# Gathered float32 rows of A, added on VectorE, for every other step of the last chunk of a graph layer

## The chip, the cores and the metric

The kernel runs on one core of one Trainium2 chip. The engines are written as the profile has them: PE is TensorE (PEld its weight loads), DVE is VectorE, ACT is ScalarE, POOL is GpSimd, SP is SyncE, which here only issues DMAs. The metric is the device time of one execution in microseconds; lower is better. The time before is 2595.76 us, the median of 3 runs (2591.33 to 2597.96).

## The reference

12500 nodes with 64 features each, 212500 edges sorted by their destination node `dst`, one weight per edge. The first layer's matrix `eW1` has 129 rows: 64 for the row node, 64 for the column node, one for the weight. H is 128.

```python
h = jnp.maximum(_layernorm(x, axis=-1), 0.0)
# row = src, col = dst, dist = edge_weight1
edge_in = jnp.concatenate([h[row], h[col], dist], axis=1)
e = jax.nn.silu(edge_in @ eW1 + eb1)
e = jax.nn.silu(e @ eW2 + eb2)
agg = jax.ops.segment_sum(e, row, num_segments=h.shape[0])
node_in = jnp.concatenate([h, agg], axis=1)
out = x + jax.nn.silu(node_in @ nW1 + nb1) @ nW2 + nb2
```

The edge layer's first product splits into a table A of h times the first 64 rows of `eW1` (taken by `src`), a table B of h times the next 64 rows (taken by `dst`), and the weight's row. The sums run over `src`, while the edges come sorted by `dst`.

## The kernel before, in words

**Tables.** `products` (L578) forms the rows of A and of B for four nodes per partition at a time, 25 times. A is written to DRAM (`ta`) as three bfloat16 parts whose sum is the float32 row (L591 to L601), B as float32 (`tb`, L594). `hd` keeps h, transposed, for the node layer (L586). This work, the "feed", is cut into pieces by `yield` and dealt out between the pieces of the next stage.

**Sorting the edges by source.** The nodes lie in 100 buckets of 125 (bucket is `src` mod 100). `send_all` takes the edges in blocks of 1024: `count` (DVE, L306 to L329) finds each edge's place in its bucket, `send` (L331 on) forms B plus the weight's part for each edge on PE (L349), copies it to SBUF on ACT (L356), and POOL scatters it by indirect DMA, 128 rows at a time, into a DRAM buffer `q` (L370). A row of `q` has 144 words: 128 of data and 16 with the edge's place in its bucket, plus one (a zero row has place zero). The edges are cut into 11 chunks; a chunk's part of `q` can only be read when all its scatters have landed. Zeros are written into the next chunk's part from ACT's queue.

**Reading back.** A batch is four buckets of one chunk: in the first chunk one step, in the ten others two steps, g = 0 and g = 1. A step handles four tiles of 128 edges. `fetch` (L405) is emitted four batches ahead, right after the `one` operation of a batch's last step, and issues on SP's queue: the tile `qt` of edges (L415, 576 KB), the rows of A for the four buckets, `a3` (L420), and in the last chunk the node layer's inputs `xr` and `hrn` (L105, L206); POOL adds a bias to `xr` (L204). The tile pool of `qt` has four buffers, so SP's issue waits until the batch four earlier has been read.

A step is a row of small functions:
- `s_lr` (PE, L438) spreads the place of each edge over the partitions; `s_one_t` (DVE, L443) compares it with the partition number, which gives a one-hot matrix `oneT`;
- `s_pt` (PE) transposes the edge rows into PSUM (L452) and adds the three parts of A times `oneT` (six matmuls, L459); ACT applies SiLU (L463);
- `s_bias` (ACT, L485), `s_p2` (PE, L491; ACT, L495): the second layer;
- `s_one` (DVE, L472) builds the one-hot matrix the other way round, and `s_seg` (PE, L505) sums with it;
- `s_add` (DVE, L516) adds the batch's sums to `aggT`.

In the last chunk the node layer follows each batch (`nodes`: PE L216, L219, L225, ACT L221, DVE L228 with `os`, SP L105).

**The order.** The work of PE, DVE, ACT and SP stands in the order in which the program emits it. In iteration k the emission is `s_pt(k+1)`, `s_add(k-2)`, `s_one_t(k+2)`, `s_bias(k+1)`, `s_p2(k)`, `s_one(k)`, `s_seg(k-1)`, `s_lr(k+3)`, with pieces of sending, feed and node layer at the four places marked `None` in `turn` (L523). POOL's order is left to the framework's scheduler.

Of the kernel before, what the change touches and what calls it, by code (L numbers as in the profile page):

```python
# [28 lines left out]
F32 = mybir.dt.float32  # L29
F16 = mybir.dt.float16  # L30
BF16 = mybir.dt.bfloat16
I32 = mybir.dt.int32
AF = mybir.ActivationFunctionType
OP = mybir.AluOpType
# [4 lines left out]
P = 128  # L39
# [7 lines left out]
G = 4  # L47
# [12 lines left out]
def tile_gnn(ctx: ExitStack, tc: tile.TileContext, x, src, dst, ew, eW1, eb1, eW2, eb2, nW1, nb1, nW2, nb2, out):  # L60
    nc = tc.nc
    N, D = x.shape
    H = eW2.shape[0]
    E = src.shape[0]
    assert D == 64 and H == P and N % L == 0
    NB = N // L
# [6 lines left out]
    const = ctx.enter_context(tc.tile_pool(name="const", bufs=1))  # L73
    dram = ctx.enter_context(tc.tile_pool(name="dram", bufs=1, space=DRAM))
# [47 lines left out]
    nc.gpsimd.iota(nodes_i, pattern=[[1, L]], base=1, channel_multiplier=0)  # L122
    nodes1 = const.tile([P, L], F32, name="nodes1")
    nc.vector.tensor_copy(nodes1, nodes_i)
    w1 = const.tile([P, 2, H], F32, name="w1")
    w1n = const.tile([P, H], F32, name="w1n")
    for a in range(2):
# [24 lines left out]
    same = const.tile([P, 1], F32, name="same")  # L152
# [11 lines left out]

    ta = dram.tile([P * NB, 3 * H], BF16, name="ta")
    tb = dram.tile([P * NB, H], F32, name="tb")
    rows = dram.tile([NP, 2, 2, BLK], BF16, name="rows")

    tb0 = dram.tile([P * NE, H], F32, name="tb0")
# [2 lines left out]
    def product(s, hr, ps, tag, to):  # L172

        abs_ = []
        for a in range(2):

            half = slice(a * D, (a + 1) * D)
            ab = ps.tile([P, G // 2, H], F32, name="ab", tag=tag)
            for i in range(G // 2):
                nc.tensor.matmul(ab[:, i], hr[half, i, :], w1[half, s, :], start=True, stop=True)  # L180
            abs_.append(ab)
        for a in range(2):
            nc.scalar.copy(to.rearrange("l (i a) h -> l a i h", a=2)[:, a], abs_[a])
# [16 lines left out]
    def nodes_in(B, sb):  # L200
        b = B * G
        xr = sb.tile([L, G, D], F32, name="xr")
        rows16(nc.sync.dma_start, xr, x_rows[:, b : b + G, :])
        nc.gpsimd.tensor_tensor(xr, xr, nb2b[:L, None, :].to_broadcast([L, G, D]), op=OP.add)  # L204
        hr = sb.tile([P, G // 2, P], F32, name="hrn")
        nc.sync.dma_start(hr, hd[:, b // 2 : b // 2 + G // 2, :])  # L206
        return xr, hr
# [31 lines left out]
    with ExitStack() as work:  # L239
# [165 lines left out]
        def fetch(i):  # L405
            if i >= len(batches):
                return
            c, B, n = batches[i]
            assert pending[c] == 0
            while B not in done_a:  # L410
                next(feed)
            q = chunks[c][-1]
            at = B * G * n * P
            qt = ld2.tile([P, G * most, W], F32, name="qt")
            nc.sync.dma_start(  # L415
                qt[:, : G * n, :].rearrange("p j w -> p (j w)"),
                q[at : at + G * n * P, :].rearrange("(p j) w -> p (j w)", p=P),
            )
            a3 = ld2.tile([P, G, 3, H], BF16, name="a3")
            nc.sync.dma_start(  # L420
                a3.rearrange("l b s f -> l b (s f)"), ta_buckets[:, B * G : B * G + G]
            )
            batch[c, B] = [qt, a3, None]
            if c == len(chunks) - 1:
                node_in[B] = nodes_in(B, ndp[0])

        def of(k):

            c, B, n, g = steps[k]
            return batch[c, B], [((g * G + t) % n * G + (g * G + t) // n, (g * G + t) // n) for t in range(G)]  # L430

        def s_lr(k):
            (qt, _, _), tiles = of(k)
            loc = qt.rearrange("p j w -> p (j w)").bitcast(BF16)
            lr = mm.tile([P, G, P], F32, name="lr", tag="mm")
            for t, (j, _) in enumerate(tiles):
                at = 2 * (j * W + H) + 1
                nc.tensor.matmul(lr[:L, t, :], loc[:, at : at + 1].to_broadcast([P, L]), identb, start=True, stop=True)  # L438
            st[k] = {"lr": lr}

        def s_one_t(k):
            oneT = wk.tile([L, G, P], BF16, name="oneT")
            nc.vector.tensor_scalar(oneT, st[k].pop("lr")[:L], part1[:L, :], None, op0=OP.is_equal)  # L443
            st[k]["oneT"] = oneT

        def s_pt(k):

            (qt, a3, _), tiles = of(k)
            oneT = st[k].pop("oneT")
            pt = mm.tile([P, G, P], F32, name="pt", tag="mm")  # L450
            for t, (j, _) in enumerate(tiles):
                nc.tensor.matmul(  # L452
                    pt[:, t, :], qt[:, j, :H], ident, is_transpose=True, start=t == 0, stop=False, skip_group_check=True
                )
            for b, same in itertools.groupby(range(G), lambda t: tiles[t][1]):
                same = list(same)
                cols = slice(same[0], same[-1] + 1)
                for i in range(3):
                    nc.tensor.matmul(  # L459
                        pt[:, cols, :], a3[:L, b, i, :], oneT[:, cols, :], start=False, stop=i == 2, skip_group_check=True  # L460
                    )
            e1 = wk.tile([P, G, P], F32, name="e1")
            nc.scalar.activation(e1, pt, AF.Silu)  # L463
            st[k]["e1"] = e1
# [52 lines left out]
            if c == len(chunks) - 1:  # L517
                tails.append(nodes(B, *node_in.pop(B), mm, ndp[1], "mm"))

        tails, node_in = [], {}  # L520


        turn = [  # L523
# [34 lines left out]
        def first_rows(g):  # L558

            hr = turned(x0, g)  # L560
            yield
            got = fp.tile([P, G, H], F32, name="got")
            product(1, hr, mm, "mm", got)
            yield
            nc.sync.dma_start(tb0.rearrange("(p j) f -> p j f", j=NE)[:, g : g + G, :], got)
            yield
# [11 lines left out]
        def products(b0, g, xs):  # L578

            assert b0 in ready  # L580
            b = b0 + g
            hr = turned(xs, g)
            yield
            rows_a = fp.tile([P, G, H], F32, name="rows_a")
            product(0, hr, mm, "mm", rows_a)
            nc.sync.dma_start(hd[:, b // 2 : (b + G) // 2, :], hr)  # L586
            yield
            got = fp.tile([P, G, H], F32, name="got")
            product(1, hr, mm, "mm", got)
            parts = fp.tile([P, G, 3, H], BF16, name="parts")  # L590
            nc.scalar.copy(parts[:, :, 0, :], rows_a)  # L591
            yield
            nc.vector.tensor_tensor(rows_a, rows_a, parts[:, :, 0, :], op=OP.subtract)
            nc.sync.dma_start(tb_buckets[:, b : b + G, :], got)  # L594
            done_b.append(b // G)
            yield
            nc.scalar.copy(parts[:, :, 1, :], rows_a)
            yield
            nc.vector.tensor_tensor(parts[:, :, 2, :], rows_a, parts[:, :, 1, :], op=OP.subtract)
            yield  # L600
            nc.sync.dma_start(ta_buckets[:, b : b + G, :], parts.rearrange("p b s f -> p b (s f)"))  # L601
            done_a.append(b // G)
            yield
# [348 lines left out]
```

## Time and profile before

| | |
|---|---|
| median of 3 runs | 2595.76 us |
| the profiled execution | 2590.2 us, its span 2588.4 us |
| busy: PE, PEld | 2205.0 us (85%), 2041.8 us (79%) |
| busy: DVE, ACT, POOL | 2034.8 us (79%), 1246.9 us (48%), 1736.8 us (67%) |
| mean granted clock of PE | 0.926 |
| DMA over the span | 577.23 MB, 223 GB/s |
| POOL L370 scatters | 1661, mean 1022 ns |
| DVE L443 oneT, L472 one, L516 aggT | 525 of 744 ns, 525 of 670 ns, 250 of 667 ns |
| PE L438 lr, L459 products with A | 2100 of 225 ns, 3600 of 245 to 273 ns |

The span is the time from the first to the last recorded instruction of one execution; that execution's own time is 1.8 us longer. Matmuls overlap in PE, so a group's mean duration is longer than the step from one matmul to the next; the time that PE is held by some work is read from the starts in the timeline. "Idle before, releaser" names what ended an engine's idle time. A line of the timeline has start, duration, engine, line, operation, output and inputs with shapes, and in brackets the idle time before it.

### The profile page before, as it was taken

How to read it: one execution, taken by the hardware profiler on the slowest of the kernel's cores; microseconds unless marked ns; L12 is line 12 of the kernel's file. 1: busy time of each engine (PE TensorE's matmuls, PEld its weight loads, DVE VectorE, ACT ScalarE, POOL GpSimd, SP SyncE). 2: the span in 40 equal slices, each digit the busy share in tenths (PEclk: the TensorE clock that was granted, in tenths of full speed). 3: DMA queues.
4: the chain of work that ended last, by engine and by line, in shares of the span. 5: the costliest groups of instructions: out<-in, count | busy, mean ns of one | idle time of the engine just before them, and what ended most of it. 6: DMA issues, size and time to landing. Idle time of an engine off the chain costs nothing.

```text
span 2588.4 us, 60017 instructions
## 1 busy us (share of the span) xinstructions
PE 2205.0 (85%) x21814; PEld 2041.8 (79%) x21814; DVE 2034.8 (79%) x3464; ACT 1246.9 (48%) x2687; POOL 1736.8 (67%) x1729
## 2 busy tenths in 40 slices
PE   2456777988998998999899799889889999997997
PEld 1345667977987987888788799889879889996996
DVE  5877987987987887888788799879879889973442
ACT  2344634544554554555455455445545455553443
POOL 3675777777777777777677777777767777772000
PEclk7556888998999999999999899999989999998999
DMA  8787778669768767866966877786696667655441
GB/s 202 216 246 263 254 234 271 217 204 269 237 210 247 252 219 227 267 216 218 272 227 211 240 248 237 220 260 228 211 274 228 215 203 235 230 169 174 166 150 54
DMA packets 257977, 577.23 MB, mean 223 GB/s; under 512 B 51202, under 2 KB 110580, under 8 KB 257469
## 3 DMA queue, kind: packets, MB, share of 16 engines
q1 hardware_dynamic: 185096, 384.91, 45.7%
q0 software_dynamic: 54144, 123.04, 13.1%
q10 hardware_dynamic: 18434, 65.37, 11.4%
q8 instruction: 175, 2.87, 0.5%
q14 instruction: 128, 1.04, 0.1%
HBM read 361.44 MB, written 211.67 MB: 221 GB/s over the span
## 4 chain that ended last, share of the span: by engine, by line
PE 40%; DMA 23%; DVE 13%; POOL 7%; issue 6%; ACT 2%; SPq 1%; DVEq 0%; ACTq 0%; POOLq 0%
DMA q<-qs,to 14%; PE seg L505 10%; PE p L491 9%; POOL q L370 7%; PE pt L459 7%; PE pt L452 5%; DVE misc L317 5%; PE qp L349 4%; PE lr L438 3%; DMA bc<-rows 2%; DVE oneT L443 2%; DMA bb<-rows 2%; DVE one L472 2%; DMA pick<-in_edge_weight_dram 2%; DVE own L322 2%
## 5 line engine op out<-in xcount | busy, mean ns | idle before, releaser
L370 POOL DMA_INDIRECT q<-qs,to x1661 | 1697.4, 1022 | 602.7 <-issue 397.5
L463 ACT ACTIVATE e<-pt 128x512 f32<-128x512 f32 x525 | 313.7, 598 | 835.8 <-PE pt L459 769.6
L505 PE MATMUL seg<-one,e 128*128 128x125 f32 x4200 | 581.4, 282 | 54.7 <-DVE aggT L516 42.5
L491 PE MATMUL p<-w,e 128*128 128x128 f32 x4200 | 587.2, 284 | 5.3 <-ACT p L485 5.3
L317 DVE TENSOR_TENSOR_SCAN misc<-oh,misc 100x342 f32<-100x342 f16 (+1 forms) x623 | 579.7, 930 | 9.3 <-PE misc L341 1.2
L505 PEld LDWEIGHTS seg<-one,e 128*128 128x128 f32 x4200 | 524.4, 196 | 68.5 <-ACT p L485 27.7
L491 PEld LDWEIGHTS p<-w,e 128*128 128x128 f32 x4200 | 527.9, 197 | 31.0 <-issue 8.4
L443 DVE TENSOR_SCALAR oneT<-lr,part 125x512 bf16<-125x512 f32 x525 | 390.8, 744 | 111.1 <-PE lr L438 109.0
L459 PE MATMUL pt<-oneT,a 125*128 125x256 bf16 (+1 forms) x3300 | 443.0, 273 | 0.1
L452 PE MATMUL pt<-ident,qt 128*128 128x128 f32 x2100 | 332.0, 282 | 73.4 <-DVE oneT L443 73.4
L356 ACT COPY qs<-qp 128x512 f32<-128x512 f32 x416 | 229.2, 587 | 320.3 <-PE qp L349 225.7
L472 DVE TENSOR_TENSOR one<-nodes,qt 128x500 f32<-128x500 f32 x525 | 351.7, 670 | 0.7 <-PE seg L505 0.5
L459 PEld LDWEIGHTS <-a 125*128 125x128 bf16 x3300 | 318.7, 100 | 35.5 <-issue 1.0
L322 DVE TENSOR_TENSOR own<-misc,oh 100x342 f16<-100x342 f32 (+1 forms) x623 | 320.0, 514 | 21.6
L495 ACT ACTIVATE e<-p 128x512 f32<-128x512 f32 x525 | 314.1, 598 | 18.6 <-PE p L491 18.0
L485 ACT COPY p<-b2f 128x512 f32<-128x512 f32 x525 | 312.5, 595 | 0.1
L349 PE MATMUL qp<-win,pick 50*128 50x128 f32 x3322 | 260.7, 299 | 60.6 <-DMA pick<-in_edge_weight_dram 34.5
L349 PEld LDWEIGHTS qp<-win,pick 50*128 50x128 f32 x3322 | 220.4, 200 | 92.9 <-issue 71.5
L452 PEld LDWEIGHTS pt<-ident,qt 128*128 128x128 f32 x2100 | 228.3, 144 | 79.0 <-DVE oneT L443 76.3
L516 DVE TENSOR_TENSOR aggT<-aggT,seg 128x500 f32<-128x500 f32 x250 | 166.9, 667 | 94.2 <-PE seg L505 93.9
L438 PE MATMUL lr<-identb,qt 128*125 128x128 bf16 x2100 | 213.3, 225 | 30.6 <-DMA qt<-q 25.3
L438 PEld LDWEIGHTS <-qt 128*125 128x125 bf16 x2100 | 186.4, 139 | 42.1 <-DMA qt<-q 31.5
(121 smaller groups left out, 1086.3 us busy)
## 6 DMA issues: line engine op xcount, KB each, us to landing
qt<-q SPq DMA_DIRECT2D x250, 576.0 KB
a<-ta SPq DMA_DIRECT2D x275, 384.0 KB
q<-zeros ACTq DMA_DIRECT2D x30, 1638.0 KB
bb<-rows SPq DMA_DIRECT2D x208, 224.0 KB
bc<-rows SPq DMA_DIRECT2D x208, 128.0 KB
q<-qs,to POOLq DMA_INDIRECT x1661
win<-tb SPq DMA_DIRECT2D x416, 24.0 KB
ta<-parts SPq DMA_DIRECT2D x25, 384.0 KB
```

The costliest lines, as they stand in the source:

```text
L317: nc.vector.tensor_tensor_scan(run[:, :m], oh[:, cols], nil.to_broadcast([NB, m]), carry.get(c, -1.0), op0=OP.add, op1=OP.add)
L322: nc.vector.tensor_tensor(own[:, cols], run[:, :m], oh[:, cols], op=OP.mult)
L349: nc.tensor.matmul(qps[a][:, t, :], pick[half, t * P : (t + 1) * P], win[half, :], start=True, stop=True)
L370: i = nc.gpsimd.indirect_dma_start(out=q[:], out_offset=bass.IndirectOffsetOnAxis(ap=to[:k, t : t + 1], axis=0), in_=qs[:k, t - t0, :], in ...
L438: nc.tensor.matmul(lr[:L, t, :], loc[:, at : at + 1].to_broadcast([P, L]), identb, start=True, stop=True)
L443: nc.vector.tensor_scalar(oneT, st[k].pop("lr")[:L], part1[:L, :], None, op0=OP.is_equal)
L452: nc.tensor.matmul(pt[:, t, :], qt[:, j, :H], ident, is_transpose=True, start=t == 0, stop=False, skip_group_check=True)
L459: nc.tensor.matmul(pt[:, cols, :], a3[:L, b, i, :], oneT[:, cols, :], start=False, stop=i == 2, skip_group_check=True)
L472: nc.vector.tensor_tensor(one.rearrange("p (b j) l -> p b j l", j=n), nodes1[:, None, None, :].to_broadcast(wide), loc[:, tiles[0][1] : ti ...
L491: nc.tensor.matmul(p2[:, t, :], e1[:, t, :], w2, start=False, stop=t == G - 1, skip_group_check=True)
L495: nc.scalar.activation(e2, p2, AF.Silu)
L505: nc.tensor.matmul(item[2][:, b, :], e2[:, t, :], one[:, t, :], start=j < G, stop=j >= G * (n - 1))
```

## The change

For the last chunk, step g = 1 of each of its 25 batches gets the rows of A in another way.

- `products` also writes the float32 rows of A to a DRAM table `taf`. So that `rows_a` stays whole until that write has read it, the difference goes into a new tile `rest`; the tiles `got` and `rest` have two buffers (`got` had three).
- Two constants, `four_i` and `four`, are set up at the start.
- `fetch`, in the last chunk, adds two DVE operations on the location column of the tile that it has just asked for (`place`, then `idx`, the row numbers in `taf` of four tiles of edges), and four indirect DMAs on POOL, each of which gathers 128 rows of 512 bytes into `rows_of_a`.
- For such a step `s_lr` emits nothing, `s_one_t` adds `rows_of_a` to the edge rows in place on DVE, and `s_pt` only transposes.

Step g = 0 of each batch, and all other chunks, stay as they are.

```diff
--- before.py
+++ after.py
@@ -122,6 +122,10 @@
     nc.gpsimd.iota(nodes_i, pattern=[[1, L]], base=1, channel_multiplier=0)
     nodes1 = const.tile([P, L], F32, name="nodes1")
     nc.vector.tensor_copy(nodes1, nodes_i)
+    four_i = const.tile([P, G], I32, name="four_i")
+    nc.gpsimd.iota(four_i, pattern=[[1, G]], base=-NB, channel_multiplier=0)
+    four = const.tile([P, G], F32, name="four")
+    nc.vector.tensor_copy(four, four_i)
     w1 = const.tile([P, 2, H], F32, name="w1")
     w1n = const.tile([P, H], F32, name="w1n")
     for a in range(2):
@@ -164,6 +168,7 @@
 
     ta = dram.tile([P * NB, 3 * H], BF16, name="ta")
     tb = dram.tile([P * NB, H], F32, name="tb")
+    taf = dram.tile([P * NB, H], F32, name="taf")
     rows = dram.tile([NP, 2, 2, BLK], BF16, name="rows")
 
     tb0 = dram.tile([P * NE, H], F32, name="tb0")
@@ -423,6 +428,30 @@
             batch[c, B] = [qt, a3, None]
             if c == len(chunks) - 1:
                 node_in[B] = nodes_in(B, ndp[0])
+                if n > 1:
+
+                    k = steps.index((c, B, n, n - 1))
+                    _, tiles = of(k)
+                    idx = ndp[0].tile([P, G], I32, name="idx")
+                    place = ndp[0].tile([P, G], F32, name="place")
+                    b0 = tiles[0][1]
+                    loc = qt[:, : G * n, H : H + 1].rearrange("p (j b) w -> p b (j w)", b=G)[:, b0 : b0 + G // n]
+                    wide = [P, G // n, n]
+                    at = place.rearrange("p (b j) -> p b j", j=n)
+                    nc.vector.tensor_scalar(at, loc, 1.0, float(NB), op0=OP.max, op1=OP.mult)
+                    nc.vector.scalar_tensor_tensor(
+                        idx.rearrange("p (b j) -> p b j", j=n), at, float(B * G),
+                        four[:, b0 : b0 + G // n, None].to_broadcast(wide), op0=OP.add, op1=OP.add,
+                    )
+                    rows_of_a = ndp[0].tile([P, G, H], F32, name="rows_of_a")
+                    for t in range(G):
+                        nc.gpsimd.indirect_dma_start(
+                            out=rows_of_a[:, t, :],
+                            out_offset=None,
+                            in_=taf[:],
+                            in_offset=bass.IndirectOffsetOnAxis(ap=idx[:, t : t + 1], axis=0),
+                        )
+                    gathered[k] = rows_of_a
 
         def of(k):
 
@@ -431,6 +460,9 @@
 
         def s_lr(k):
             (qt, _, _), tiles = of(k)
+            if k in gathered:
+                st[k] = {}
+                return
             loc = qt.rearrange("p j w -> p (j w)").bitcast(BF16)
             lr = mm.tile([P, G, P], F32, name="lr", tag="mm")
             for t, (j, _) in enumerate(tiles):
@@ -439,6 +471,12 @@
             st[k] = {"lr": lr}
 
         def s_one_t(k):
+            if k in gathered:
+                (qt, _, _), tiles = of(k)
+                n = steps[k][2]
+                q = qt[:, : G * n, :H].rearrange("p (j b) w -> p b j w", b=G)[:, tiles[0][1] : tiles[0][1] + G // n]
+                nc.vector.tensor_tensor(q, q, gathered[k].rearrange("p (b j) w -> p b j w", j=n), op=OP.add)
+                return
             oneT = wk.tile([L, G, P], BF16, name="oneT")
             nc.vector.tensor_scalar(oneT, st[k].pop("lr")[:L], part1[:L, :], None, op0=OP.is_equal)
             st[k]["oneT"] = oneT
@@ -446,13 +484,14 @@
         def s_pt(k):
 
             (qt, a3, _), tiles = of(k)
-            oneT = st[k].pop("oneT")
             pt = mm.tile([P, G, P], F32, name="pt", tag="mm")
             for t, (j, _) in enumerate(tiles):
                 nc.tensor.matmul(
-                    pt[:, t, :], qt[:, j, :H], ident, is_transpose=True, start=t == 0, stop=False, skip_group_check=True
+                    pt[:, t, :], qt[:, j, :H], ident, is_transpose=True, start=t == 0,
+                    stop=k in gathered and t == G - 1, skip_group_check=True,
                 )
-            for b, same in itertools.groupby(range(G), lambda t: tiles[t][1]):
+            oneT = st[k].pop("oneT", None)
+            for b, same in [] if k in gathered else itertools.groupby(range(G), lambda t: tiles[t][1]):
                 same = list(same)
                 cols = slice(same[0], same[-1] + 1)
                 for i in range(3):
@@ -517,7 +556,7 @@
             if c == len(chunks) - 1:
                 tails.append(nodes(B, *node_in.pop(B), mm, ndp[1], "mm"))
 
-        tails, node_in = [], {}
+        tails, node_in, gathered = [], {}, {}
 
 
         turn = [
@@ -559,7 +598,7 @@
 
             hr = turned(x0, g)
             yield
-            got = fp.tile([P, G, H], F32, name="got")
+            got = fp.tile([P, G, H], F32, name="got", bufs=2)
             product(1, hr, mm, "mm", got)
             yield
             nc.sync.dma_start(tb0.rearrange("(p j) f -> p j f", j=NE)[:, g : g + G, :], got)
@@ -583,20 +622,22 @@
             yield
             rows_a = fp.tile([P, G, H], F32, name="rows_a")
             product(0, hr, mm, "mm", rows_a)
+            nc.sync.dma_start(taf.rearrange("(l b) f -> l b f", b=NB)[:, b : b + G, :], rows_a)
             nc.sync.dma_start(hd[:, b // 2 : (b + G) // 2, :], hr)
             yield
-            got = fp.tile([P, G, H], F32, name="got")
+            got = fp.tile([P, G, H], F32, name="got", bufs=2)
             product(1, hr, mm, "mm", got)
             parts = fp.tile([P, G, 3, H], BF16, name="parts")
             nc.scalar.copy(parts[:, :, 0, :], rows_a)
             yield
-            nc.vector.tensor_tensor(rows_a, rows_a, parts[:, :, 0, :], op=OP.subtract)
+            rest = fp.tile([P, G, H], F32, name="rest", bufs=2)
+            nc.vector.tensor_tensor(rest, rows_a, parts[:, :, 0, :], op=OP.subtract)
             nc.sync.dma_start(tb_buckets[:, b : b + G, :], got)
             done_b.append(b // G)
             yield
-            nc.scalar.copy(parts[:, :, 1, :], rows_a)
-            yield
-            nc.vector.tensor_tensor(parts[:, :, 2, :], rows_a, parts[:, :, 1, :], op=OP.subtract)
+            nc.scalar.copy(parts[:, :, 1, :], rest)
+            yield
+            nc.vector.tensor_tensor(parts[:, :, 2, :], rest, parts[:, :, 1, :], op=OP.subtract)
             yield
             nc.sync.dma_start(ta_buckets[:, b : b + G, :], parts.rearrange("p b s f -> p b (s f)"))
             done_a.append(b // G)
```

## The prediction

> **What bounds the kernel now.** I first read the busy time by stretch (columns: length, then busy us and instruction count of PE, PEld, DVE, ACT, POOL; then granted PE clock, DMA share, GB/s).
>
> ```profile
> 200.00:220.00 20.00, 6.52 (x52) 5.44 (x52) 9.94 (x17) 5.67 (x16) 8.38 (x8) 0.50 0.89 311
> 1000.00:2000.00 1000.00, 900.89 (x9118) 841.99 (x9119) 846.67 (x1428) 496.28 (x1062) 747.02 (x738) 0.96 0.76 238
> 2300.00:2340.00 40.00, 27.29 (x264) 26.18 (x262) 14.66 (x27) 14.90 (x30) 30.55 (x32) 0.87 0.33 108
> 2340.00:2588.00 248.00, 228.09 (x1951) 205.89 (x1951) 95.34 (x157) 103.18 (x204) 19.03 (x26) 0.96 0.43 140
> ```
>
> POOL's scatters run at one per 1.27 us (0.97 busy, 0.30 "issue"), which is a busy share of 0.76; it has 0.75 in the middle and 0.76 just before 2340. So scatter issue paces the kernel until 2340. From there PE is busy 92%, and POOL and DVE have room: the edited stretch is bound by PE. In the first stretch shown POOL is at half its pace with DMA at 0.89; I come back to it.
>
> Next, the timeline at the seam to the last chunk, and what SP's queue waits for (window 2300 to 2590):
>
> ```profile
> 2307.56 0.16 DVE L361 SCALAR_TENSOR_TENSOR to<-misc,bkE 128x5 int32<-128x5 f32 x1 [1.96 <-DMA q<-qs,to]
> 2307.64 0.67 DVE L472 TENSOR_TENSOR one<-nodes,qt 128x500 f32<-128x500 f32 x1
> ...
> 2313.02 0.67 DVE L472 TENSOR_TENSOR one<-nodes,qt 128x500 f32<-128x500 f32 x1
> ...
> 2326.24 1.05 PE L505 MATMUL seg<-one,e 128*128 128x125 f32 x8
> ...
> 2341.29 0.32 SPq L415 DMA_DIRECT2D qt<-q  x1
> ...
> 2345.71 0.50 PEld L438 LDWEIGHTS <-qt 128*125 128x125 bf16 x4 [18.61 <-DMA qt<-q]
> ```
> ```profile
> SPq L415 <- DVE one L472: 110.3, 24, 6.1
> SPq L415 <- DMA q<-qs,to: 30.9, 1, 30.9
> ```
>
> The `one` at 2313.02 belongs to the step after which the load for batch 0 of the last chunk (I write B0) is emitted. That load sits in SP's queue 30.9 us until the last scatter has landed, is issued at 2341.29, and its data release PE at 2345.71: 4.42 us. Meanwhile PE and DVE work on through three more batches, to 2327.3. In later rounds SP issues the load at once when `one` ends.
>
> Then one batch of the PE-bound stretch:
>
> ```profile
> 2407.60 0.68 DVE L516 TENSOR_TENSOR aggT<-aggT,seg 128x500 f32<-128x500 f32 x1 [1.54 <-PE seg L505]
> ...
> 2408.20 0.74 DVE L443 TENSOR_SCALAR oneT<-lr,part 125x512 bf16<-125x512 f32 x1
> ...
> 2408.86 0.67 DVE L472 TENSOR_TENSOR one<-nodes,qt 128x500 f32<-128x500 f32 x1
> ...
> 2409.59 0.34 SPq L415 DMA_DIRECT2D qt<-q  x1
> ...
> 2413.05 0.39 PE L438 MATMUL lr<-identb,qt 128*125 128x128 bf16 x4
> ...
> 2413.28 0.61 PE L452 MATMUL pt<-ident,qt 128*128 128x128 f32 x4
> ...
> 2413.73 0.82 PE L459 MATMUL pt<-oneT,a 125*128 125x256 bf16 x6
> ...
> 2414.38 1.06 PE L491 MATMUL p<-w,e 128*128 128x128 f32 x8
> ```
>
> Loads follow each other 8.76 us apart (2400.83, 2409.59): that is the round of a batch.
>
> **What is removed from PE.** By starts in those lines, four lr take 0.23 us (2413.05 to 2413.28) and six products with A 0.65 (2413.73 to 2414.38): 0.88 us per batch, 22 us over 25 batches. PE's round would become 7.88. DVE gives up one oneT (0.74) for an add of 128x512 f32; the nearest rows, one and aggT, have 0.67, and I take that. This is the whole possible gain.
>
> **What is added, and where it queues.** After the load, fetch now puts two small DVE operations that read the location column of the tile just being loaded. The rows u (0.15) and to (0.16) are the nearest: 0.31 us of work. But they wait for the load to land, and DVE takes its work in the order written: in the first pair of lines above `to` waits 1.96 us for a DMA, and `one` starts right behind it. So everything behind these two stands still for the whole load: os, oneT, one, aggT and the new add of the next two steps; PE waits for oneT, and the next load waits for the `one` that comes last in this list. Issue, landing and DVE's work make a closed ring, which does not exist now.
>
> The ring's length: two small ones 0.31, os 0.42, oneT 0.74, two one 1.34, aggT 0.68, new add 0.67 = 4.16. DVE's starts lie about 0.08 closer than its durations (2408.20 to 2408.86 for 0.74), six times: 3.68, plus 0.06 from one's end to the issue: about 3.75 us. To this comes the load, call it L.
>
> L in the trace, by the bytes that queue q1 had moved from just before the issue (0.59 MB is the tile). Windows 2400.8 to 2403.5, to 2403.75, without scatters; then 2301.7 to 2305, to 2305.5, with scatters beside it:
>
> ```profile
> q1 hardware_dynamic: 118, 0.54, 62.1%
> q1 hardware_dynamic: 151, 0.62, 64.0%
> ...
> q1 hardware_dynamic: 107, 0.49, 61.2%
> q1 hardware_dynamic: 166, 0.67, 65.2%
> ```
>
> Without scatters 0.59 MB is there at 2403.66, 2.83 us after the issue at 2400.83; with them at 2305.28, 3.56 after 2301.72. At the seam it was there at 2344.39 and PE went at 2345.71, so the end signal takes 1.32. L is 4.15 alone and 4.88 beside scatters. The gathers are such neighbours: four per batch at 1.27 us, after the xr add on POOL, about 2 to 7 us after a landing, while the next load is in flight from 3.75 to 8.4. No gather is in this trace; from below it costs nothing (4.15), from above I double the scatters' surcharge (5.6). I take 4.7, near the scatter row, since most of the load is overlapped and the rows are a little smaller.
>
> The ring is then 3.75 + 4.7 = 8.45 us, against 8.76 now and 7.88 for PE alone. So in the steady rounds a third of the gain is left: 0.31 us.
>
> A rule against the row: the Trainium skill, "DMA: Bandwidth & Descriptors", section "Anatomy of one DMA — SWDGE (gpsimd) path", fits a DMA by 2.0 us plus its bytes at 436 GB/s, 3.35 us for this tile (my estimate from it, for another path than this load's). By that the ring would be 7.1 us, hidden under PE's 7.88, and the change of the total about -5 us; the trace's 4.42 and 4.15 speak against it.
>
> **The seam.** DVE now stops behind the `one` of 2313.02 until 2345.7. PE comes as far as the lr three steps ahead, about 2318.2, and the work it did from there to 2327.3 is left for afterwards, 9 us. From 2345.7 the rounds are serial: 0.31 + oneT 0.67 + one 0.6 + aggT 0.6 + oneT 0.67 + one 0.67 puts the next issue at 2349.3 and its landing at 2354.0; the two small ones, five more operations and 4.7 give 2362.3; then 2370.5, 2378.7 (rounds of 8.2, no os yet). The transposes of batch B2 start after the small ones and oneT, at 2379.8, against 2363.8 now: 16.0 us late. PE's half clock after the gap (0.50 in the rows until 2350) is paid before and after alike.
>
> From there 20 rounds with a load each win 0.31: -6.2. The last three batches have no load to wait for and win PE's part: -2.4. Sum for the last chunk: 16.0 - 6.2 - 2.4 = +7.4 us.
>
> POOL's own work is covered: four gathers and xr are 5.8 us of an 8.4 us round, and each is used three batches later.
>
> **The early part.** 25 writes of A's f32 table (256 KB each) join SP's queue ahead of hd; behind each stand the bc, bb, win and pick loads. From 76 to 320 us DMA moved 59.49 MB at 244 GB/s; 6.4 MB more is 26 us if all of it were bound there, none if covered. POOL is short of work only around 160 to 240 (8.38 in the row above, against 15.3 at its pace), with some 7 of the 25 writes; I take half their DMA time, 7 x 1.05 / 2, about +4. Two buffers for got in place of three, and the new tile rest, only matter if a tb write is slow (one wait of 7.5 us in the trace); they stay in the range. The two constants cost 0.2 us at the start, covered by its loads.
>
> **Sum.** +7.4 + 4 = +11.4 us. On the profiled execution (2590.2, span 2588.4) that is 2601.6; that execution lies 5.6 below the median of the runs, 2595.76, so the forecast is 2607.2.
>
> **Rivals.**
> 1. The gathers crowd the load: L 5.6, ring 9.35. The seam becomes 16.0 + 4 x 0.9 = 19.6, twenty rounds +11.8, -2.4, +4: +33, 2629. For it: 512 more packets of only 512 bytes in each round. Against: scatters added only 0.73.
> 2. The gathers are harmless: L 4.15, ring 7.90, level with PE. 16.0 - 2.2 - 17.2 - 2.4 + 4: -2, 2594.
> 3. Faster: DVE's queue isn't held, because the two small ones find their tile landed or stand behind other work. Then no ring and no seam: -22 + 4 = -18, 2577.8. It decides only if the load is shorter than what DVE has to do ahead of them; the trace has nothing between `one` and the issue but 0.06 us, so I give it little.
> 4. The table writes cost the full 26: 2629, from a DMA share already at 0.9; against it, POOL is short of work in few stretches.
> That a gathered step is skipped silently I rule out: its tile is entered at least five steps before lr is built for it.
>
> **Chances.** The forecast, L from 4.4 to 5.0 (2600 to 2615): 0.50. Rival 1: 0.15. Rival 2: 0.15. Rival 3: 0.15. Rival 4: 0.05. What a measurement can tell from no change is 0.3%, 7.8 us: below 2588 or above 2603.5. Rival 3 gives faster, 0.15. Rival 2 and the lower part of the forecast (0.08) are the same, 0.23. The rest, 0.62, is slower. The range leaves out rival 3 and a little above rivals 1 and 4: 2589 to 2634.
>
> **What would show it.** DVE idle of about 4 to 5 us per batch before the place operation, ended by DMA qt<-q; one of about 32 us at the seam; loads 8.2 to 8.7 apart; PE no longer dense after 2350 but waiting for DVE oneT; and the last scatter landing within 0 to 10 us of 2341. If PE stays dense with rounds of 7.9, the ring is wrong; if the rounds are as said and the total still differs, the early part is.

## The result, and the profile after

The changed kernel takes 2597.1 us (median of 22 runs, 2589.65 to 2602.59). The kernel before takes 2590.43 us in the same comparison (22 runs, 2587.09 to 2597.96). The ratio is 1.002 with a 95% interval of 1.0011 to 1.0028: slower, by 5 us (the two medians lie 6.7 apart), and inside the 0.3% that the prediction called no change. The profiled execution took 2596.03 us, its span is 2594.3 us against 2588.4.

The last scatter, after which no stretch of the two kernels is paced by POOL any more, cuts the span in two. It starts at 2339.20 us before and at 2350.52 us after:

```profile
2339.20 0.89 POOL L370 DMA_INDIRECT q<-qs,to  x1 [0.31 <-issue]
```
```profile
2350.52 0.89 POOL L375 DMA_INDIRECT q<-qs,to  x1 [0.31 <-issue]
```

| stretch | before | after | difference | forecast |
|---|---|---|---|---|
| start to the last scatter | 2339.2 | 2350.5 | +11.3 | +4 |
| last scatter to the end | 249.2 | 243.7 | -5.5 | +7.4 |
| span | 2588.4 | 2594.3 | +5.8 | +11.4 |

So the last chunk became shorter, and the work ahead of it gave more than that back.

First the waits of the changed kernel from 2300 to 2594 us (who waited for what: total, times, longest):

```profile
DVE place L441 <- DMA qt<-q: 130.1, 25, 31.1
PE pt L498 <- DVE oneT L481: 31.2, 5, 27.2
```

DVE does stand still at `place` (L441), once for each of the 25 loads. One of these waits is the seam: 31.1 us, in which PE gets no `oneT`. The timeline shows the seam and its first rounds (start, duration, engine, line, operation, idle time before it):

```profile
2352.62 0.32 SPq L420 DMA_DIRECT2D qt<-q  x1
...
2356.31 0.17 DVE L441 TENSOR_SCALAR place<-qt 128x4 f32<-128x4 f32 x1 [31.08 <-DMA qt<-q]
...
2357.39 1.44 PE L498 MATMUL pt<-oneT,a 125*128 125x256 bf16 x6 [27.23 <-DVE oneT L481]
...
2359.82 0.34 SPq L420 DMA_DIRECT2D qt<-q  x1
...
2363.65 0.26 DVE L441 TENSOR_SCALAR place<-qt 128x4 f32<-128x4 f32 x1 [3.89 <-DMA qt<-q]
```

From the issue at 2352.62 to `place` at 2356.31 the load takes 3.69 us; the next one takes 3.83 (2359.82 to 2363.65). A later round, DVE alone, where the ring can be read from end to end:

```profile
2474.56 0.17 DVE L441 TENSOR_SCALAR place<-qt 128x4 f32<-128x4 f32 x1 [4.43 <-DMA qt<-q]
2474.76 0.16 DVE L442 SCALAR_TENSOR_TENSOR idx<-place,four 128x4 int32<-128x4 f32 x1
2474.87 0.42 DVE L233 TENSOR_TENSOR os<-o,xr 125x256 f32<-125x256 f32 x1
2475.21 0.74 DVE L481 TENSOR_SCALAR oneT<-lr,part 125x512 bf16<-125x512 f32 x1
2475.87 0.67 DVE L511 TENSOR_TENSOR one<-nodes,qt 128x500 f32<-128x500 f32 x1
2476.46 0.67 DVE L555 TENSOR_TENSOR aggT<-aggT,seg 128x500 f32<-128x500 f32 x1
2477.05 0.68 DVE L478 TENSOR_TENSOR qt<-qt,rows_of_a 128x512 f32<-128x512 f32 x1
2477.65 0.67 DVE L511 TENSOR_TENSOR one<-nodes,qt 128x500 f32<-128x500 f32 x1
2482.24 0.17 DVE L441 TENSOR_SCALAR place<-qt 128x4 f32<-128x4 f32 x1 [3.92 <-DMA qt<-q]
```

All eight operations that the prediction listed lie between two waits, in the order in which it listed them: the ring is there, 7.68 us long in this round. Over the last 20 loads the load is 4.07 us in the mean (3.56 to 5.12). The last 19 rounds, from issue to issue, are 8.02 us in the mean, so the rest of a round is 3.95.

This mean hides two kinds of rounds. In the nine whose load took 4.06 us or more, the trace shows no wait of DVE between `place` and the next issue; that stretch is 3.79 to 3.83 us, and the round is the load plus that, 7.89 to 8.91. In the ten with a shorter load it is 3.89 to 4.26: `aggT` comes late there and in five of them waits 0.20 to 0.34 us for PE's `seg`, and the round is 7.81 to 7.89. So the ring sets the pace in about half of the rounds, and PE in the other half.

The stretches that answer to those of before (columns as in the prediction):

```profile
200.00:220.00 20.00, 8.84 (x74) 7.44 (x73) 12.39 (x22) 6.47 (x21) 6.99 (x8) 0.50 0.95 318
1000.00:2000.00 1000.00, 892.97 (x9036) 833.99 (x9035) 837.74 (x1415) 490.38 (x1049) 749.22 (x737) 0.96 0.75 236
2350.00:2594.00 244.00, 217.73 (x1783) 194.63 (x1782) 104.13 (x217) 108.07 (x213) 122.53 (x127) 0.95 0.55 169
```

In the last row PE has 89% where it had 92%, so it is not as dense as before, and POOL has its hundred gathers. The row of the middle is nearly unchanged. In the first row the share of DMA went from 0.89 to 0.95, and POOL from 8.38 to 6.99 us of 20.

The matmuls `z` of the node layer (PE L221, L216 before) come once per batch and mark the rounds. From the first to the 23rd of them it is 176.2 us after (2388.72 to 2564.90, 8.01 per batch) and 192.8 before (2364.91 to 2557.73, 8.76). So the 5.5 us of the last chunk come out as follows: from the last scatter to the first `z` 38.2 us against 25.7, +12.5; 22 rounds -16.6; the rest 29.4 against 30.7, -1.3.

The kernels that take the early part to pieces, and the one without gathers, ran on three other chips where every kernel, the one before included, took about 3470 us in place of 2590; their ratios are to runs of the kernel before on the same chip.

### The profile page after: what moved, and what is told of

Read it like the earlier page. It is cut to its first block, busy times and chain, and to the rows that moved or that the text cites. A ratio compares the mean times of both kernels' runs of the same rounds, so it can differ in the third digit from the quotient of the medians.

```text
span 2594.3 us, 59640 instructions
## 1 busy us (share of the span) xinstructions
PE 2190.2 (84%) x21564; PEld 2027.6 (78%) x21564; DVE 2035.3 (78%) x3515; ACT 1247.1 (48%) x2687; POOL 1845.2 (71%) x1830
## 3 DMA queue, kind: packets, MB, share of 16 engines
q0 software_dynamic: 57344, 129.60, 14.1%
q8 instruction: 173, 2.83, 0.5%
HBM read 367.99 MB, written 218.23 MB: 226 GB/s over the span
## 5 line engine op out<-in xcount | busy, mean ns | idle before, releaser
L375 POOL DMA_INDIRECT q<-qs,to x1661 | 1703.1, 1025 | 607.9 <-issue 406.7
L530 PEld LDWEIGHTS p<-w,e 128*128 128x128 f32 x4200 | 527.0, 197 | 25.7 <-issue 8.3
L498 PE MATMUL pt<-oneT,a 125*128 125x256 bf16 (+1 forms) x3150 | 426.4, 275 | 31.3 <-DVE oneT L481 31.2
L481 DVE TENSOR_SCALAR oneT<-lr,part 125x512 bf16<-125x512 f32 x500 | 372.0, 744 | 81.0 <-PE lr L470 71.7
L498 PEld LDWEIGHTS <-a 125*128 125x128 bf16 x3150 | 306.7, 101 | 66.6 <-issue 33.1
L470 PE MATMUL lr<-identb,qt 128*125 128x128 bf16 x2000 | 204.6, 226 | 21.5 <-DMA qt<-q 21.4
L470 PEld LDWEIGHTS <-qt 128*125 128x125 bf16 x2000 | 178.9, 140 | 32.7 <-DMA qt<-q 22.1
```

The lines of the kernel that those rows point to most:

```text
L375: i = nc.gpsimd.indirect_dma_start(out=q[:], out_offset=bass.IndirectOffsetOnAxis(ap=to[:k, t : t + 1], axis=0), in_=qs[:k, t - t0, :], in ...
L498: nc.tensor.matmul(pt[:, cols, :], a3[:L, b, i, :], oneT[:, cols, :], start=False, stop=i == 2, skip_group_check=True)
L530: nc.tensor.matmul(p2[:, t, :], e1[:, t, :], w2, start=False, stop=t == G - 1, skip_group_check=True)
```

## The experiments

My theory after the result: in the last chunk the ring is right and only its load was priced too high, and the price of the part ahead of it is that of the 25 new writes. Rivals: the ring costs nothing any more, since PE's rounds became as long; the gathers set the load's length; ahead of the last chunk, not the bytes of the writes but SP's wait for them, or the new buffers.

**Each half alone.** The first kernel has the early part of the change with the last chunk as it was:

```diff
-                if n > 1:
+                if False:
```

> The changed kernel with its early part alone: the float32 table is written in the feed, rest and two buffers for got are there, but nothing is gathered and the last chunk runs as before. Theory (the loss comes from the early part): the last scatter is issued some 11 us later than before's 2339, the stretch after it is before's 249 us, and the time is 10 to 12 us above before. Rival (the forecast's own split): +4 us here, and the rest in the last chunk.

It took 2598.1 us, against 2589.17 of the kernel before on that chip (23 runs): ratio 1.0036, 1.0021 to 1.0052. Its last scatter starts at 2353.32, and from there to the end it needs 248.3 us, as the kernel before does (249.2). So the early part costs about 9 us by itself, and the rest of the change can't be what delays the last scatter.

Its seam also repeats the load from which the prediction took its end signal, with the next load 2.21 us behind it as in the kernel before:

```profile
2355.42 0.32 SPq L420 DMA_DIRECT2D qt<-q  x1
...
2357.63 0.36 SPq L420 DMA_DIRECT2D qt<-q  x1
...
2359.15 0.50 PEld L470 LDWEIGHTS <-qt 128*125 128x125 bf16 x4 [17.92 <-DMA qt<-q]
```

It takes 3.73 us here, where the trace of before has 4.42.

The second has the last chunk's part alone; `products` is as before and no table is written, so the gathers read `tb`:

```diff
-    taf = dram.tile([P * NB, H], F32, name="taf")
...
-                            in_=taf[:],
+                            in_=tb[:],
...
-            nc.sync.dma_start(taf.rearrange("(l b) f -> l b f", b=NB)[:, b : b + G, :], rows_a)
```

> The changed kernel without its early part: no float32 table; the gathers read the rows of the table tb, which has the same shape, so the work and its order in the last chunk are the same but the gathered steps get rows of B in place of rows of A. Theory: the last scatter is at before's 2339, the stretch after it is 244 us as in the changed kernel, and the time is 4 to 7 us below before. Rival (the forecast's split): 7 us above before.

2580.01 us, ratio 0.9965 (0.9947 to 0.9983): faster than before. From the last scatter (2332.99) to the end it takes 242.1 us, 7.1 less than before, with the same wait, from 2300 us on (in both runs the rival, the forecast's own split, is out):

```profile
DVE place L440 <- DMA qt<-q: 128.1, 25, 31.1
```

By the times the halves are +9 us (5 to 14) and -9 (-14 to -4); the whole, +5, lies within what these two allow together. Between the two traces, 6.2 us of the gain lie ahead of the last scatter (2332.99 against 2339.20), where this kernel does the work of the one before; no run explains them. The traces are sharper: the stretch from the last scatter on is 242.1 and 243.7 us with the gathers, 248.3 and 249.2 without.

The traces also tell when the early part costs. In the changed kernel the 25 new writes are issued from 88.9 to 322.3 us. Three pairs of kernels from chips at 2590 us differ, up to the last chunk, in the early part alone. Start of the 241st scatter, and of the last:

| pair, with the early part against without | 241st scatter | last scatter |
|---|---|---|
| early part alone, before | 434.9, 421.5: +13.4 | 2353.3, 2339.2: +14.1 |
| changed kernel, last chunk's part alone | 430.0, 418.5: +11.5 | 2350.5, 2333.0: +17.5 |
| the two kernels with the late `idx`, below | 430.9, 417.3: +13.6 | 2333.9, 2312.1: +21.8 |

So 11 to 14 us are lost by about 430 us, while the tables are made and shortly after. What is added later, 0.7 to 8.2 us, differs from pair to pair.

**The ring taken away.** `place`, `idx` and the gathers are emitted one batch after their load (for the first batch two batches later); nothing else changes:

```diff
-                if n > 1:
+                later.append((248 if B == 0 else i - NQ + 1, lambda: gather(c, B, n)))
...
+                at = c * (NB // G) + B
+                while later and later[0][0] <= at:
+                    later.pop(0)[1]()
-                fetch(c * (NB // G) + B + NQ)
+                fetch(at + NQ)
```

> The changed kernel with one thing moved: the two index operations and the four gathers of a batch are emitted one batch later (for the first batch of the last chunk two batches later), so that DVE reaches them when the tile has landed. Theory (DVE's queue was held for the whole load): DVE no longer waits for the load in the steady rounds, PE goes on to 2337 before the seam, the rounds are 7.9 us, and the stretch after the last scatter is 249 - 22 + 0 to 4 = 227 to 231 us; with the early part's +11 the time is 7 to 11 us below before. Rival (PE's work was the bound of the rounds in the changed kernel anyway, and the wait only filled spare time of DVE): the stretch stays at 240 us or more and the time within 3 us of the changed kernel.

2569.03 us, ratio 0.9913 (0.9892 to 0.9935). From the last scatter (2333.91) to the end it takes 234.5 us, 9.3 less than the changed kernel and 14.7 less than before. The 234.5 us are more than the theory's 227 to 231 and less than the rival's 240. The time is 20 us below before, where 7 to 11 were expected; the surplus lies ahead of the last scatter (last section). The waits from 2300 us on, then a round of its timeline:

```profile
DVE place L446 <- DMA qt<-q: 20.7, 3, 16.2
DVE qt L483 <- DMA rows_of_a<-taf,idx: 10.9, 3, 6.5
```
```profile
2420.60 0.68 DVE L483 TENSOR_TENSOR qt<-qt,rows_of_a 128x512 f32<-128x512 f32 x1
2422.33 0.16 DVE L446 TENSOR_SCALAR place<-qt 128x4 f32<-128x4 f32 x1
2422.47 0.34 SPq L420 DMA_DIRECT2D qt<-q  x1
2422.52 0.16 DVE L447 SCALAR_TENSOR_TENSOR idx<-place,four 128x4 int32<-128x4 f32 x1
```

`place` reads a tile that landed long before and starts without a wait; the load is issued 0.14 us behind it and holds up nobody. The `z` matmuls now come every 7.87 to 7.88 us, PE's own round. That settles two things. The forecast's figure for PE alone, 7.88, was right. And the stop behind the load still cost something in the changed kernel, but little in the rounds: 22 times 0.13 us is 3 us, where the seam gives 6.4 (from the last scatter to the first `z` 31.8 us in place of 38.2). It still isn't the 25.7 of before: DVE waits at the seam for the rows of the first gathers, up to 6.5 us in the second line above.

**The gathers taken away, the ring kept.**

```diff
-                    rows_of_a = ndp[0].tile([P, G, H], F32, name="rows_of_a")
-                    for t in range(G):
-                        nc.gpsimd.indirect_dma_start(
...
+                    rows_of_a = zeros[:, : G * H].rearrange("p (t w) -> p t w", t=G)
```

> The changed kernel without its 100 gathers; VectorE adds a tile of zeros of the same size in their place, so the output lacks those rows. The load of the qt tile then runs beside SP's own transfers alone. If gathers and loads share DMA time, the load falls from the 3.7 to 4.2 us that most rounds show to 3.5 or less and a double step from 7.90 to about 7.3 us, so that the last chunk is 15 us shorter (time about 2582). If the load's length is its own, it stays at 4 us, VectorE's ring stays at 7.8 us or more, and the time is within 4 us of the changed kernel's 2597.

This ran on one of the chips at 3470 us (ratio to before 1.0002, 0.9986 to 1.0019), so the expectation on the time has no answer. The last chunk's own rows can be read: PE's granted clock is 0.97 there, and a round looks like the others:

```profile
3332.83 0.17 DVE L441 TENSOR_SCALAR place<-qt 128x4 f32<-128x4 f32 x1 [3.79 <-DMA qt<-q]
...
3336.98 0.34 SPq L420 DMA_DIRECT2D qt<-q  x1
3340.70 0.17 DVE L441 TENSOR_SCALAR place<-qt 128x4 f32<-128x4 f32 x1 [3.79 <-DMA qt<-q]
```

The load is 3.72 us here, 3.73 in the mean of the last 20. So the gathers lengthen it by 0.34 us (4.07 - 3.73). The two means come from different chips, but the traces at 2590 us agree: of their six first loads at the seam, which no gather accompanies, five took 3.69 to 3.82 us, and the sixth is the 4.42 of before. Neither expectation was met in full. The load fell less than the first one said and more than the second, and the rounds hardly shortened: `place` comes every 7.91 us over the last 19 rounds, against 8.04 with the gathers, because PE's 7.87 is next in line.

**What in the early part costs.** The first four kernels on this leave the last chunk as before, like the early part alone, and take pieces from it: without the 25 writes (the new tile `rest` and the two buffers of `got` kept); each write cut to one of 128 partitions, SP's wait kept; writes of full size from a tile of zeros, so without that wait; and the write moved behind that of `tb`.

```diff
-            nc.sync.dma_start(taf.rearrange("(l b) f -> l b f", b=NB)[:, b : b + G, :], rows_a)
+            nc.sync.dma_start(taf.rearrange("(l b) f -> l b f", b=NB)[:1, b : b + G, :], rows_a[:1])
```
```diff
-            nc.sync.dma_start(taf.rearrange("(l b) f -> l b f", b=NB)[:, b : b + G, :], rows_a)
+            nc.sync.dma_start(
+                taf.rearrange("(l b) f -> l b f", b=NB)[:, b : b + G, :], zeros[:, : G * H].rearrange("p (g h) -> p g h", g=G)
+            )
```

> The early part without the table's write: rest, two buffers for got and the two constants stay; nothing is gathered, the last chunk is before's. Theory W (the write costs, by the wait of SP's queue or by its bytes): within 3 us of before. Theory B (two buffers for got in place of three hold the feed up): 6 to 10 us above before, as the whole early part.

> The early part with the write cut to one partition's row (2 KB in place of 256 KB): SP's queue still waits there for ACT's copies of rows_a, but almost no bytes move. Theory Q (SP's queue is held, with the bc, bb, win and pick loads behind it): 6 to 10 us above before, and SP's wait at this line 25 us or more from 60 to 420 us. Theory D (the 6.4 MB of DMA work cost): within 3 us of before.

> The early part with a write of the same size at the same place, whose source is a tile of zeros that has long been there: all the bytes move, but SP's queue waits for nothing at this line. Theory D: 6 to 10 us above before. Theory Q: within 3 us of before.

> The early part with the same write of rows_a moved behind the write of got to tb, which SP waits for anyhow and which ACT finishes later than rows_a: all the bytes, no wait of its own. Theory Q: 0 to 4 us above before, SP's wait at the moved line near none. Theory D: 6 to 10 us above.

Three of them on a second such chip, and on a third one beside the whole early part (the copies on ACT that some of these texts name are in the kernel before as well):

> The early part without its 25 writes of table rows (the last chunk with products as before, the copies of A's rows into float32 kept). If the wait or the bytes of the writes make the early part's cost, the time is that of the kernel before within 0.1% (2590 us, 2587 to 2593), and 230 scatters or more have begun by 400 us less two. If something else in the early part makes it (the copies on ACT, the second buffer of rows), 9 us stay: 2599 us, ratio 1.0036 as in the run with the early part alone. The run of the same kernel on a chip where every kernel took 3470 us could not tell these apart (1.0015, 0.9985 to 1.0045).

> The early part with each write of table rows cut to one of 128 partitions: SP waits for ACT's rows as before, 1/128 of the bytes go out. If the wait in SP's queue makes the cost, 2599 us (ratio 1.003 to 1.004), with some 25 us of SP's time at the write in the first 420 us. If the bytes make it, 2590 us (1.000) with the same wait.

> The early part with writes of the same size from a tile of zeros that is ready from the start: all the bytes, no wait for ACT's rows at the write. If the wait makes the cost, 2590 us (1.000); if the bytes make it, 2599 us (1.003 to 1.004). A part of each gives 2593 to 2596.

> The early part alone, whole: A's rows copied into float32, the 25 writes of table rows in SP's queue, the last chunk's products as before. It gave 1.0036 (1.0021 to 1.0052) on a chip where the kernel before took 2589 us; the same is expected here, as the measure for the other three.

> The early part without the 25 writes. If the writes make the cost, by their wait or their bytes, 1.000 and 116 scatters or more begun at 250 us (117 in the kernel before, 113 with the change, 112 with the early part whole). If the copies or the second buffer make it, 1.0036 and 112 or 113.

> Each write cut to one of 128 partitions, SP's wait for ACT's rows kept. If the wait makes the cost, 1.003 to 1.004 and 112 to 113 scatters at 250 us; if the bytes, 1.000 and 116 to 117.

> Writes of full size from a tile of zeros, without the wait for ACT's rows. If the wait makes the cost, 1.000 and 116 to 117 scatters at 250 us; if the bytes, 1.003 to 1.004 and 112 to 113.

All of them met chips at 3470 us. Ratios to the kernel before, and the scatters in the first 250 us of each profile, counted in one stretch (the 117, 113 and 112 of the expectations were added up from short stretches, where one on an edge counts twice; in one stretch they are 114, 108 and 107):

| early part | ratio (95% interval) | scatters by 250 us |
|---|---|---|
| whole | 1.0028 (1.0002 to 1.0054) | 99 |
| no writes | 1.0015 (0.9985 to 1.0045), 1.0051 (1.0029 to 1.0072), 1.0013 (0.9983 to 1.0044) | 103, 104, 101 |
| wait, 1/128 of the bytes | 1.0025 (0.9994 to 1.0056), 1.0015 (0.9988 to 1.0042), 1.0022 (0.9993 to 1.0052) | 101, 102, 99 |
| bytes, no wait for ACT's rows | 1.0012 (0.9984 to 1.0041), 1.0018 (0.9993 to 1.0042), 1.0039 (1.0007 to 1.0071) | 98, 98, 99 |
| write behind that of `tb` | 1.0052 (1.0025 to 1.0078) | 100 |

The times tell nothing apart: the intervals overlap, and the three runs without writes lie as far from each other as from the whole. On such a chip POOL is idle ahead of its scatters two and a half times as long as in the kernel before at 2590 us (602.7 us there). The line is from the groups of the last run of the cut write (busy us, mean ns, idle time before):

```profile
L375 POOL DMA_INDIRECT q<-qs,to x1661 | 1670.8, 1006 | 1514.3 <-ACT qs L370 786.9
```

A few scatters that are late early on may vanish in that idle time. From 60 to 420 us SP's queue waits 38 to 45 us at the cut write (43 at the write of the whole early part on such a chip), so the wait was kept; with the tile of zeros it still waits 24 to 25 us at the write of `hd` behind it, so only part of the wait was taken away. The counts at 250 us lean toward the bytes, but they overlap: 98 to 99 with all the bytes and no wait, 99 to 102 with the wait and hardly any bytes, 101 to 104 with neither, and 99 for the whole.

The traces from chips at 2590 us tell the early part as a whole apart, not the writes from the buffers. With it, 108 scatters fall into the first 250 us (the changed kernel), 107 (early part alone) and 108 (ring taken away); without it 114 (before), 116 (last chunk's part alone) and 116 (the last kernel below). SP's waits from 60 to 420 us show that its queue is held by little more than it was. Before, then after:

```profile
SPq L586 <- ACT qs L365: 13.5, 6, 9.1
SPq L594 <- ACT got L183: 11.2, 6, 4.5
```
```profile
SPq L625 <- ACT rows_a L188: 25.6, 9, 12.4
SPq L625 <- DMA q<-zeros: 7.6, 1, 7.6
SPq L635 <- ACT got L188: 2.5, 1, 2.5
```

The new write (L625) takes over waits that the writes of `hd` and `tb` had. All waits of SP at the writes of A, `hd` and B come to 53.0 us after (L625 40.1, L635 5.9, L642 7.0) and 47.5 before (L586 19.5, L594 16.2, L601 11.8). That speaks for the bytes and against the wait; no run shows it in the time, and none shows in the time that it is the writes and not the new buffers.

**Without the table.** The bfloat16 rows in `ta` hold the same numbers. This kernel has the late `idx` of above, gathers 768 bytes a row from `ta`, adds the three parts in three DVE operations, and writes no table; `products` is as before.

```diff
-                            in_=taf[:],
+                            in_=ta[:],
...
-                nc.vector.tensor_tensor(q, q, gathered[k].rearrange("p (b j) w -> p b j w", j=n), op=OP.add)
+                for i in range(3):
+                    part_i = gathered[k][:, :, i, :].rearrange("p (b j) w -> p b j w", j=n)
+                    nc.vector.tensor_tensor(q, q, part_i, op=OP.add)
```

> Index and gathers late as in the run before, and no float32 table: the gathers read the 768-byte rows of the three bfloat16 parts from the table that is there already, and DVE adds the three parts one after the other (two adds more per batch, 1.4 us). Early part as before the change. Theory: no early loss, rounds of 7.9 us since DVE's work of some 5.2 us per batch fits in; 17 to 22 us below before. Rival (the longer gathers or the two adds become the bound): rounds of 8.5 us or more, 5 us below before or less.

2553.55 us, ratio 0.9865 (0.9841 to 0.9889): it beats both kernels. Its last scatter starts at 2312.15, and the rest takes 236.9 us, 2.4 more than with one add. The rounds are as the theory said; the time is 36 us below before, where 17 to 22 were expected. PE does not pay for the two more additions, since DVE is no longer in a ring: `z` comes every 7.87 to 7.88 us, and the 2.4 us are lost at the seam, where the first `z` starts 34.3 us after the last scatter (2346.41) in place of 31.8. What the kernel gains over the one before comes mostly ahead of the seam (27.0 us of it in the traces, 12.4 behind), where its work is that of the kernel before; that part is not explained (last section).

## Why the prediction was right or wrong

Point by point, in its order:

- **What bounds the last chunk, and PE's gain.** Right. PE alone makes 7.87 us a round where the ring is gone; 7.88 was worked out from starts in the trace of before.
- **DVE's queue is held for the whole load.** Right: 25 waits at `place`, ended by the load, and the next load waits for the `one` behind it. Rival 3, in which it isn't held, is what the kernel with the late `idx` became by an edit.
- **The seam's stall.** 31.08 us at `place`, where about 32 was said. Its price was 12.5 us instead of 16.0: each of the first rounds was shorter than forecast (7.2 to 7.6 us from load to load, against 8.0 to 8.2). That is the load again: the first five took 19.8 us together (3.69, 3.83, 3.98, 4.17, 4.16) where the forecast had 23.2 (4.42 and four of 4.7), 3.4 less.
- **The ring's length: the term that was mis-sized in the last chunk.** The prediction took 4.7 us for the load L, between 4.15 and 5.6. It is 4.07 beside the gathers and 3.73 without them, below the lower end. DVE's share, 3.75, was 3.82 where DVE did not wait. With the measured mean of the load the prediction's own ring is 3.75 + 4.07 = 7.82 us, level with PE's 7.88, and what the ring still costs comes from the rounds with a longer load. So a round is 8.02 in place of 8.45 us, 0.15 above PE's, and 22 rounds give 16.6 us where 6.2 was forecast for 20. The lower end was itself a sum of two rows: bytes counted in one load (2.83 us) and an end signal of 1.32 us from the load at the seam, 4.42 us long. That one load was an exception. With the early part alone the load at the same place, with the same next load 2.21 us behind it, took 3.73 us and its end signal, counted in the same way, 0.8; with the late `idx` it took 3.74 and 3.82. So it wasn't the next load that made it long; why it took longer in the one trace of before is open.
- **The rule against the row.** The Trainium skill, "DMA: Bandwidth & Descriptors", section "Anatomy of one DMA — SWDGE (gpsimd) path", gives 3.35 us for this tile, as an estimate from its fit. The load measured 3.73 us without gathers, nearer to the fit than to the 4.42 us that the prediction set against it. It speaks of another path than this load's.
- **Rival 2**, harmless gathers with a ring of 7.90, was the better case for the last chunk: -5.8 there by its terms, -5.5 measured. The gathers are not quite harmless (0.34 us of the load), but the load is short enough to carry them.
- **The early part: the second mis-sized term.** +4 was taken, half the DMA time of the 7 writes in the starved stretch; it was +11.3 between the two traces, +9 in the times of the early part alone, and +11 to +14 by the 241st scatter in the three pairs above. The bounds, 0 and 26, held it. The choice of 7 writes was too narrow: six scatters are missing at 250 us already (108 against 114), eight at 2300 us (1622 against 1630).
- **The sum.** Two errors of opposite sign, -12.9 in the last chunk and +7.3 ahead of it, half cancel; with only one of them the total would be -1.5 or +18.7, so that it came as near to the forecast as it did (+5.8 against +11.4 between the traces) is luck. The forecast of 2607.2 also stood on the median of 3 runs, 2595.76, which lies 5.3 us above that of 22. The result lies in the range (2589 to 2634), but in the case "within 0.3%", to which 0.23 was given, and not in "slower by over 0.3%", which had 0.62.

What stays open: whether the writes or the new buffers cost the 9 to 14 us, and, if the writes, whether by their bytes or by the wait. And see the last section on when the last scatter comes.

## What to carry to other kernels

An operation that reads a tile just asked for, put on an in-order engine that also does the work that frees the next tile, ties the two into a ring; emit it one batch later, when its tile has landed, and the ring is gone and with it half of the delay at the seam (6.4 of 12.5 us here). Price a load from several loads and not from one (4.42 us here, where five others of its kind took 3.69 to 3.82), and when a bound is itself a sum of two rows from different loads, carry a wider one. Before writing a new table from a stretch that is bound by DMA, look for one that exists already: here two more additions per step, on an engine with room, cost 2.4 us, and the whole early part with the table's 6.6 MB (HBM written: 218.23 MB after, 211.67 before) 9 us or more.

## What the runs showed of the hardware that was not expected

The two kernels with the late `idx` reach their last scatter earlier than their twins: 2333.91 against 2350.52 with the table, 2312.15 against 2332.99 without it. Up to the last chunk the instructions are the same in each pair. At the 241st scatter the late kernels are level with their twins (+0.9 and -1.2 us), and the lead grows over the rest of the span. POOL's scatters (1661 in each) are busy for 1682.8 us in place of 1703.1, and 1680.4 in place of 1693.2; the median of one is 958 ns in the two late kernels and 967 ns in the four others at 2590 us, which over 1661 scatters is 15 us. No run tells why the same instruction takes 9 ns less there, nor whether that is all of the lead. So some of the gain of these two kernels (0.9913 and 0.9865) is not from the edit of the last chunk; what is from it is read from the stretch behind the last scatter, -14.7 and -12.4 us.
